# 64-row parts of q, k and v in one group per token tile, and the weights of k issued sooner, in a transformer block

## The chip, the cores and the metric

The kernel runs on one core of a Trainium2 chip. The metric is the device time of one execution in microseconds; the median of several runs is given.

## What is computed

The block works on two sequences (B = 2) of 2048 tokens with 576 features, 16 heads of 36, in float32. Cut to what matters here:

```python
xn = _ln(x, 1e-06)
xn = xn * (1 + sc_msa[:, None, :]) + sh_msa[:, None, :]
qkv = (xn @ w_qkv + b_qkv).reshape(B, N, 3, H, hd)
q, k, v = (qkv[:, :, 0], qkv[:, :, 1], qkv[:, :, 2])
q = _ln(q, 1e-05, qn_g, qn_b)
k = _ln(k, 1e-05, kn_g, kn_b)
attn = softmax(einsum('bqhd,bkhd->bhqk', q, k) * hd ** (-0.5))
o = einsum('bhqk,bkhd->bqhd', attn, v).reshape(B, N, C) @ w_proj + b_proj
x = x + g_msa[:, None, :] * o
# ... then a second normalisation, a two-layer MLP and its gated residual
```

The shifts, scales and gates come from silu(c) @ w_ada + b_ada.

## The kernel before, in words

The two sequences (batches) are taken one after the other. For each there is a stage that makes q, k and v (`inputs`), a stage of attention (`attend`), and a stage of the output projection (`outputs`); the MLP of both follows at the end. The change is in `inputs` and in what it calls.

**Tiles and products.** `inputs` goes over 16 token tiles of 128 tokens. A tile's normalised rows lie in `xnt` by feature: 576 features are four chunks of 128 and one of 64, and the last chunk is there twice, in rows 0 to 63 and 64 to 127. Each of q, k and v is a product of 128 tokens by 576 columns, in two halves of 288 columns, each half in a PSUM bank of its own. `whole` (matmul at line 379) does the four full chunks of both halves, and in the trace it is 16 instructions, since a float32 matmul has two. `halved` (line 390) does the 64-row chunk: the first half on rows 0 to 63, the second on rows 64 to 127, four instructions that run in pairs side by side. `two_products` (line 394) puts them in turn: products with an even number do `whole` and then `halved`, odd ones `halved` and then `whole`, so that the 64-row parts of two neighbours come together.

**The rest of a tile.** For each tile t the loop at line 946 does q, k and v with `two_products`. VectorE adds the bias `bq` while it takes the result out of PSUM (line 960 for q and k into `both`, line 967 for v). After q it does `head_scale` of tile t-1 (line 892: a reduction on VectorE, a square root on ScalarE, a reciprocal, and a multiplication on GpSimd). After k in even tiles, and after q in odd ones, come three things: `input_by_feature` (line 851), which transposes the normalised rows of tile t+1 on TensorE (lines 357, 358) and modulates them on ScalarE (line 365); `by_feature` of tile t-2 (line 910), nine transposes of q and k (line 915), taken out of PSUM by VectorE and ScalarE; and `next_rows` (line 941), which loads and normalises tile t+2 (`rows_normed`, line 269, with a square root on ScalarE in its midst). At the end of the tile `centred` (line 877) subtracts the mean of each head on VectorE and squares on ScalarE.

**Order and buffers.** The stage has four PSUM buffers of two banks (`s_tile`, line 86). A tile takes six: q, k, v, one for the transposes of the next tile, two for `by_feature`. VectorE keeps the order of the program in this stage (line 1176); the order of the other engines is set by a scheduler by program order and readiness, and it also picks which buffer an allocation takes. After tiles 3, 7, 11, 13 and 15, `by_feature` gathers a block of keys with DMAs on SP's queue (`take_k_block`, line 806), and VectorE works on it (`parted`, line 787) in the `by_feature` that follows.

**Weights.** `input_weights` (line 825) loads them on SP's queue: q in two parts, then the 64-row chunk of all three, then x tiles 1 and 2 of batch 0 (the argument `then`, given at line 1172), the bias `bq`, k, and v. For batch 1 it is called ahead of `outputs` of batch 0, with no x tiles.

Of the kernel before, what the change touches and what calls it, by code (L numbers as in the profile page):

```python
# [8 lines left out]
F32 = mybir.dt.float32  # L9
# [3 lines left out]
ALU = mybir.AluOpType  # L13
# [3 lines left out]
P = 128  # L17
# [5 lines left out]
FULL = 4  # L23
# [8 lines left out]
def dit_block(  # L32
# [25 lines left out]
    nc = tc.nc  # L58
# [27 lines left out]
    def s_tile():  # L86
        return psum["s"].tile([P, 2, 512], F32, tag="s", name="s")
# [35 lines left out]
    def halves(ap):  # L123
        return ap.rearrange("p (a f) -> p a f", a=2)
# [224 lines left out]
        nc.vector.tensor_copy(xn[:, C:], xn[:, 512:576])  # L349
        return xn[:, :512], xn[:, 512:]  # L350

    def transposed(src, tail):

        ps = s_tile()
        t4, t1 = ps[:, 0, :], ps[:, 1, :]
        for k in range(FULL):
            nc.tensor.transpose(t4[:, k * P : (k + 1) * P], src[:, k * P : (k + 1) * P], ident)  # L357
        nc.tensor.transpose(t1[:, :P], tail, ident)  # L358
        return t4, t1

    def modulated(dst, src, which, b):

        t4, t1 = transposed(*src)
        for k in range(NKC):
            nc.scalar.activation(  # L365
                dst[:, k, :],
                t4[:, k * P : (k + 1) * P] if k < FULL else t1[:, :P],
                AF.Identity,
                bias=mod[:, which, k, b : b + 1],
                scale=mod[:, which + 1, k, b : b + 1],  # L370
            )
# [15 lines left out]
    def halved(outs, stationary, moving, first):  # L387
        for a in range(2):
            r = slice(64 * a, 64 * a + 64)
            nc.tensor.matmul(  # L390
                outs[a], stationary(FULL, a)[r], moving(FULL, a)[r], start=first, stop=not first
            )

    def two_products(outs, stationary, moving, turn):


        parts = (whole, halved) if turn % 2 == 0 else (halved, whole)
        for part in parts:
            part(outs, stationary, moving, part is parts[0])
# [325 lines left out]
    def block_of_small():  # L725
# [96 lines left out]
            for a in range(2):  # L822
                nc.sync.dma_start(out=dst[64 * a : 64 * a + 64, :, :], in_=src[:, :, a, :])

        def input_weights(then=lambda: None):
            pool, close = opened("wq")
            wq = pool.tile([P, FULL, 3 * C], F32, name="wq")
            wq4 = pool.tile([P, 3, HALF], F32, name="wq4")
            bq = pool.tile([P, 3 * C], F32, name="bq")
            for f0, n in ((0, HALF), (HALF, HALF), (C, C), (2 * C, C)):  # L830
                f = slice(f0, f0 + n)
                nc.sync.dma_start(out=wq[:, :, f], in_=w_qkv[0:512, f].rearrange("(k p) f -> p k f", p=P))
                if f0 == HALF:
                    last_chunk(wq4, w_qkv, 3, HALF)
                    then()
                    nc.sync.dma_start(out=bq, in_=b_qkv.partition_broadcast(P))
            return (wq, wq4, bq), close

        def tile_loaded(src, queue):
            xt = xs["tiles"].pop(0)  # L840
            xs["tiles"].append(xt)
            queue.dma_start(out=xt[:, :C], in_=src)
            return xt
# [4 lines left out]
        def input_rows(b, t, queue):  # L848
            return tile_normed(tile_loaded(x[b, t * P : (t + 1) * P, :], queue))

        def input_by_feature(b, rows):
            xnt = xs["pool"].tile([P, NKC, P], F32, name="xnt", bufs=2)
            modulated(xnt, rows, 0, b)
            return xnt

        def first_modulated():
# [11 lines left out]
        def inputs(b, weights, work, xnt, loaded):  # L868
# [5 lines left out]
            def banks_of_two():  # L874
                return [bank for ps in (s_tile(), s_tile()) for bank in (ps[:, 0], ps[:, 1])]
# [16 lines left out]
            def head_scale(t, both, parts=((0, 2),)):  # L892
                var = work.tile([P, 2 * H], F32, name="var")
                for w0, w1 in parts:
                    nc.vector.tensor_reduce(
                        var[:, w0 * H : w1 * H],
                        squares["sq"][:, w0 * C : w1 * C].rearrange("p (h d) -> p h d", d=HD),
                        AX.X,
                        ALU.add,
                    )  # L900
                nc.scalar.activation(var, var, AF.Sqrt, bias=eps5, scale=1.0 / HD)
                inv = work.tile([P, 2 * H], F32, name="inv")
                nc.vector.reciprocal(inv, var)
                heads = both.rearrange("p (h d) -> p h d", d=HD)
                nc.gpsimd.tensor_tensor(
                    heads, heads, inv.unsqueeze(2).to_broadcast([P, 2 * H, HD]), ALU.mult
                )
                normed[t] = both

            def by_feature(t, banks, chunks=range(NQK), all_on_vector=False):  # L910
                both, begun = normed[t], [*taken]
                taken.clear()
                parts = [(c, banks[i // 4][:, i % 4 * P : i % 4 * P + P]) for i, c in enumerate(chunks)]
                for c, ps in parts:
                    nc.tensor.transpose(ps, both[:, c * P : (c + 1) * P], ident)  # L915

                for c, ps in parts[::-1]:
                    dst = chunk(c, slice(t * P, (t + 1) * P))
                    if c < 4 and not all_on_vector:
                        nc.scalar.activation(  # L920
                            dst, ps, AF.Identity, bias=bias_qk[:, c : c + 1], scale=gain_qk[:, c : c + 1]
                        )
                    else:
                        nc.vector.tensor_scalar(
                            dst, ps, gain_qk[:, c : c + 1], bias_qk[:, c : c + 1], ALU.mult, ALU.add
                        )
                for do in begun:
                    do()
                if t == TPB - 1:
                    taken.append(take_q(0, 0))  # L930
                if t + 1 in key_tiles and NQK - 1 in chunks:
                    i = key_tiles.index(t + 1)
                    taken.append(take_k_block(*key_tiles[i - 1 : i + 1]))
# [7 lines left out]
            def next_rows(t):  # L941
                return tile_normed(loaded.pop(0)) if loaded else input_rows(b, t, nc.sync)

            rows = next_rows(1)
            before = None
            for t in range(NT):
                both = work.tile([P, 2 * C], F32, name="both", bufs=3)
                for w in range(3):
                    ps = s_tile()
                    two_products(  # L950
                        [ps[:, a, :HALF] for a in range(2)],
                        lambda k, a: xnt[:, k, :],
                        lambda k, a: (
                            wq[:, k, w * C + a * HALF : w * C + (a + 1) * HALF] if k < FULL else wq4[:, w, :]
                        ),
                        3 * t + w,
                    )
                    bias = halves(bq[:, w * C : (w + 1) * C])
                    if w < 2:
                        nc.vector.tensor_tensor(  # L960
                            halves(both[:, w * C : (w + 1) * C]), ps[:, :, :HALF], bias, ALU.add
                        )
                        if w == 0 and t > 0:
                            head_scale(t - 1, before)
                    else:
                        heads = "p a (h d) -> p a h d"
                        nc.vector.tensor_tensor(
                            vv[:, t, :, 0:HD].rearrange("p (a h) d -> p a h d", a=2),
                            ps[:, :, :HALF].rearrange(heads, d=HD),
                            bias.rearrange(heads, d=HD),  # L970
                            ALU.add,
                        )

                    if w == (1 if t % 2 == 0 else 0):
                        if t + 1 < NT:
                            ahead = input_by_feature(b, rows)
                        if t >= 2:
                            by_feature(t - 2, banks_of_two())
                        if t + 2 < NT:
                            rows = next_rows(t + 2)  # L980

                    if t == NT - 1 and w < 2:
                        centred(both, w, w + 1)
                    if t == NT - 1 and w == 1:
                        head_scale(t, both, ((0, 1), (1, 2)))
                if t + 1 < NT:
                    centred(both)
                before, xnt = both, ahead
# [119 lines left out]
        def outputs(b, weights, between, scratch):  # L1108
# [60 lines left out]
        xnt = first_modulated()  # L1169
        loaded = []  # L1170
        weights, close_weights = input_weights(
            lambda: loaded.extend(tile_loaded(x[0, t * P : (t + 1) * P, :], nc.sync) for t in (1, 2))
        )
        for b in range(B):
            work, close_work = opened("work", side="right")
# [439 lines left out]
```

## Time and profile before

| | us |
|---|---|
| median of 3 runs | 3229.54 |
| lowest and highest | 3227.64, 3229.89 |
| the profiled execution, its own time | 3230.55 |
| its span in the profile | 3228.7 |
| TensorE busy with matmuls | 3205.6 |
| line 379 in all, with wq | 392.9 |
| line 390 in all, with wq | 59.6 |

The profile names each group of instructions by line, engine and operation, with the tile written, the tiles read, the shape and the count. "Busy" counts matmuls from the start to an end that is modelled, and they overlap: the distance between two starts says what one costs. A row of the order of time has its start, its duration, the instruction and its count, and in brackets how long the engine was idle before and what released it. The q, k, v stage of batch 0 starts with line 379 at 19.83 us, that of batch 1 at 1117.97 us.

### The profile page before, as it was taken

To read this page: it belongs to the slowest core of one execution; us is meant where nothing else is said; L and a number is where in the kernel's file an instruction comes from. 1 tells how busy PE (TensorE), PEld (TensorE's weight loads), DVE (VectorE), ACT (ScalarE), POOL (GpSimd) and SP (SyncE) were. 2 spreads that over 40 slices of the span, in tenths; PEclk is the share of its full clock that TensorE was granted. 3 is DMA by queue.
4 is the path that set the end of the run, shared out by engine and by line. 5 is a ranking of instruction groups with operands and counts; after the bars stand their busy time and mean duration, and the time that the engine had idled before them with its cause. 6 is when DMAs were issued, how large, how long until landed. Compare 5 with 4: busy or idle time off the path is not lost.

```text
span 3228.7 us, 46968 instructions
## 1 busy us (share of the span) xinstructions
PE 3205.6 (99%) x18143; PEld 1883.0 (58%) x18143; DVE 1451.2 (45%) x2131; ACT 1496.8 (46%) x2952; POOL 355.1 (11%) x432
## 2 busy tenths in 40 slices
PE   8999999999999999999999999999999999999999
PEld 5775333333333777733333333358888888777777
DVE  4674333333333366633333333345555544455454
ACT  2335666666666033366666666633555552000000
POOL 1111000112110111100001111010000000111111
PEclk9999999999999999999999999999999999999999
DMA  3112212223231400122222223154322223433331
GB/s 131 26 26 65 76 35 68 66 70 83 69 85 34 146 26 24 27 56 46 50 44 65 68 66 74 47 173 156 120 90 88 93 80 110 153 132 111 118 103 38
DMA packets 129332, 253.16 MB, mean 78 GB/s; under 512 B 22979, under 2 KB 68492, under 8 KB 127052
## 3 DMA queue, kind: packets, MB, share of 16 engines
q1 hardware_dynamic: 105588, 182.07, 18.5%
q0 software_dynamic: 22640, 66.23, 7.4%
q8 instruction: 145, 2.38, 0.3%
q10 hardware_dynamic: 872, 1.77, 0.2%
q14 instruction: 87, 0.71, 0.1%
HBM read 135.40 MB, written 66.35 MB: 62 GB/s over the span
## 4 chain that ended last, share of the span: by engine, by line
PE 99%; DMA 1%; SPq 0%; DVE 0%; issue 0%; DVEq 0%
PE b L1025 28%; PE b L1012 19%; PE s L379 16%; PE s L1527 15%; PE m L1368 12%; PE s L390 2%; PE m L1382 2%; PE one L1368 2%; PE s L915 1%; PE s L357 1%; PE t L1428 0%; DMA wq<-in_w_qkv_dram 0%; DMA wa<-in_w_ada_dram 0%; PE b L192 0%; PE b L915 0%; DMA km<-qo 0%
## 5 line engine op out<-in xcount | busy, mean ns | idle before, releaser
L1016 ACT ACTIVATE pt<-b 128x512 f32<-128x512 f32 x2048 | 1057.4, 608 | 485.6 <-PE b L1025 270.8
L1025 PE MATMUL b<-pt,vt 128*64 128x512 f32 x4096 | 935.0, 598 | 0.0
L1025 PEld LDWEIGHTS b<-pt,vt 128*64 128x64 f32 x4096 | 271.9, 136 | 582.0 <-issue 438.8
L1012 PE MATMUL b<-qm,km 32*128 32x512 f32 x4096 | 566.5, 614 | 0.2 <-DMA km<-qo 0.2
L1073 DVE TENSOR_TENSOR ot<-b,ot 128x512 f32<-128x512 f32 x192 | 132.8, 691 | 653.2 <-PE b L1025 652.7
L1012 PE MATMUL b<-qe,ke 16*128 16x512 f32 x2048 | 422.8, 790 | 0.0
L379 PE MATMUL s<-wq,xnt 128*128 128x288 f32 x1536 | 392.9, 411 | 3.9 <-DMA wq<-in_w_qkv_dram 3.2
L1527 PE MATMUL s<-ws,as 128*128 128x288 f32 x1440 | 351.8, 406 | 0.0
L1012 PEld LDWEIGHTS b<-qm,km 32*128 32x128 f32 x4096 | 191.6, 184 | 269.3 <-ACT pt L1016 205.0
L379 PEld LDWEIGHTS s<-wq,xnt 128*128 128x128 f32 x1536 | 286.4, 191 | 95.5 <-issue 18.9
L1527 PEld LDWEIGHTS s<-ws,as 128*128 128x128 f32 x1440 | 273.6, 190 | 75.6
L1044 DVE RECIPROCAL den<-den 128x512 f32<-128x512 f32 x64 | 213.6, 3337 | 12.3 <-DMA den<-den_dram 12.3
L1368 PE MATMUL m<-xnt,wb 128*128 128x256 f32 x864 | 213.8, 383 | 0.0
L1368 PE MATMUL m<-s,wb 128*128 128x256 f32 x864 | 210.1, 379 | 0.2 <-DVE s L1338 0.2
L1071 DVE COPY ot<-b 128x512 f32<-128x512 f32 x64 | 44.3, 692 | 334.7 <-PE b L1025 334.7
L1368 PEld LDWEIGHTS m<-xnt,wb 128*128 128x128 f32 x864 | 159.1, 190 | 32.2 <-issue 11.9
L1368 PEld LDWEIGHTS m<-s,wb 128*128 128x128 f32 x864 | 164.1, 190 | 22.9 <-DVE s L1338 0.6
L1012 PEld LDWEIGHTS b<-qe,ke 16*128 16x128 f32 x2048 | 108.1, 184 | 114.4 <-issue 113.0
L1395 DVE TENSOR_TENSOR cs<-m,cs 128x512 f32<-128x512 f32 x72 | 49.7, 690 | 213.1 <-ACT cs L1394 151.7
L1527 PE MATMUL s<-ws,hidden 128*128 128x288 f32 x576 | 142.3, 406 | 0.0
L1505 DVE TENSOR_TENSOR as<-hidden 128x1152 f32<-128x1152 f32 x80 | 139.0, 1801 | 0.0
L365 ACT ACTIVATE xnt<-s,mod 128x128 f32<-128x128 f32 x180 | 66.8, 460 | 152.7 <-PE s L358 152.7
(174 smaller groups left out, 2553.5 us busy)
## 6 DMA issues: line engine op xcount, KB each, us to landing
gelu<-cs SPq DMA_DIRECT2D x144, 256.0 KB
hidden<-gelu SPq DMA_DIRECT2D x16, 2304.0 KB
den<-den_dram SPq DMA_DIRECT2D x128, 128.0 KB
x_dram<-kr POOLq DMA_DIRECT2D x48, 288.0 KB, 2.8
qm<-qo SPq DMA_DIRECT2D x192, 64.0 KB
kr<-in_x_dram POOLq DMA_DIRECT2D x32, 288.0 KB, 3.8
xr<-x_dram SPq DMA_DIRECT2D x32, 288.0 KB
out_dram<-y POOLq DMA_DIRECT2D x30, 288.0 KB, 3.8
```

Source lines behind the costliest of these rows:

```text
L365: nc.scalar.activation(dst[:, k, :], t4[:, k * P : (k + 1) * P] if k < FULL else t1[:, :P], AF.Identity, bias=mod[:, which, k, b : b + 1], ...
L379: nc.tensor.matmul(outs[a], stationary(k, a), moving(k, a), start=(first and k == 0), stop=(not first and k == FULL - 1),)
L390: nc.tensor.matmul(outs[a], stationary(FULL, a)[r], moving(FULL, a)[r], start=first, stop=not first)
L1012: nc.tensor.matmul(ps, k[r, keys], q[r, :], start=first, stop=not first)
L1016: nc.scalar.activation(pt[:, h, :], banks[2 * c + h], AF.Exp, scale=SCALE)
L1025: nc.tensor.matmul(acc[64 * h : 64 * h + 64, :], vt[:, v0 : v0 + 64], pt[:, h, :], start=pt is pts[0][0], stop=pt is pts[-1][0],)
L1044: nc.vector.reciprocal(den, den)
L1073: nc.vector.tensor_tensor(ot, acc, ot, ALU.add)
L1368: nc.tensor.matmul(out_m[m], wb[:, slot[m], k, f * P : (f + 1) * P], moving[m](k), start=k == 0 and (m == 1 or (first and m in (2, 5, 6))) ...
L1382: nc.tensor.matmul(out_m[m], w[r, f * P : (f + 1) * P], a[r, FULL, t * PAIR : (t + 1) * PAIR], start=first and m != 4, stop=not first and ...
L1505: nc.vector.tensor_tensor(stationary[m], x_, y_, op)
L1527: nc.tensor.matmul(ms[m], stationary[m][:, f, :], ws[m][:, f, :], start=(f == 0), stop=(f == HF - 1))
```

## The change

Tiles 0 to 13 get a loop of their own. In it q does `whole`; the transposes of the next tile follow; k does `whole`; then the three `halved` parts of q, k and v come one after the other; and v does `whole`. In tile 0 of batch 0 k's `whole` stands ahead of the transposes. `next_rows` comes right after the transposes, `head_scale` after the biases of q and k, and `by_feature` of tile t-2 after v's bias, at the end of the tile. Tiles 14 and 15 keep the old order. In four tiles (0 and 9 of batch 0, 0 and 1 of batch 1) the fifth transpose gets a PSUM buffer of its own (`apart`). In `input_weights`, k's weights are issued ahead of x tile 1, `bq` and x tile 2, which keep that order among themselves and stand ahead of v's weights.

```diff
-    def transposed(src, tail):
+    def transposed(src, tail, apart=False):
         ps = s_tile()
-        t4, t1 = ps[:, 0, :], ps[:, 1, :]
+        t4, t1 = ps[:, 0, :], (s_tile() if apart else ps)[:, 1, :]
...
                 nc.sync.dma_start(out=wq[:, :, f], in_=w_qkv[0:512, f].rearrange("(k p) f -> p k f", p=P))
                 if f0 == HALF:
                     last_chunk(wq4, w_qkv, 3, HALF)
-                    then()
+                if f0 == C:
+                    then(1)
                     nc.sync.dma_start(out=bq, in_=b_qkv.partition_broadcast(P))
+                    then(2)
...
-            for t in range(NT):
+            for t in range(NT - 2):
+                both = work.tile([P, 2 * C], F32, name="both", bufs=3)
+                q, q_parts = product(0, xnt)
+                whole(*q_parts, True)
+                behind = b == t == 0
+                if behind:
+                    k, k_parts = product(1, xnt)
+                    whole(*k_parts, True)
+                ahead = input_by_feature(b, rows, t in ((0, 9), (0, 1))[b])
+                rows = next_rows(t + 2)
+                if not behind:
+                    k, k_parts = product(1, xnt)
+                    whole(*k_parts, True)
+                v, v_parts = product(2, xnt)
+                halved(*q_parts, False)
+                halved(*k_parts, False)
+                halved(*v_parts, True)
+                biased(0, q, t, both)
+                biased(1, k, t, both)
+                if t > 0:
+                    head_scale(t - 1, before)
+                whole(*v_parts, False)
+                biased(2, v, t, both)
+                if t >= 2:
+                    by_feature(t - 2, banks_of_two())
+                centred(both)
+                before, xnt = both, ahead
+            for t in range(NT - 2, NT):
                 both = work.tile([P, 2 * C], F32, name="both", bufs=3)
                 for w in range(3):
-                    ps = s_tile()
-                    two_products(
...
+                    ps, parts = product(w, xnt)
+                    two_products(*parts, 3 * t + w)
+                    biased(w, ps, t, both)
+                    if w == 0:
+                        head_scale(t - 1, before)
```

`product` allocates a PSUM buffer and gives the halves with their operands; `biased` is the bias step that stood in the loop.

More of the change, by code (lines that the diff above doesn't have):

```diff
@@ L359, in transposed, with modulated @@
         return t4, t1
-    def modulated(dst, src, which, b):
-        t4, t1 = transposed(*src)
+    def modulated(dst, src, which, b, apart=False):
+        t4, t1 = transposed(*src, apart)
         for k in range(NKC):
@@ L823, in last_chunk, with input_weights @@
                 nc.sync.dma_start(out=dst[64 * a : 64 * a + 64, :, :], in_=src[:, :, a, :])
-        def input_weights(then=lambda: None):
+        def input_weights(then=lambda t: None):
             pool, close = opened("wq")
@@ L849, in input_rows, with input_by_feature @@
             return tile_normed(tile_loaded(x[b, t * P : (t + 1) * P, :], queue))
-        def input_by_feature(b, rows):
+        def input_by_feature(b, rows, apart=False):
             xnt = xs["pool"].tile([P, NKC, P], F32, name="xnt", bufs=2)
-            modulated(xnt, rows, 0, b)
+            modulated(xnt, rows, 0, b, apart)
             return xnt
@@ L942, in next_rows, with product, biased @@
                 return tile_normed(loaded.pop(0)) if loaded else input_rows(b, t, nc.sync)
+            def product(w, xnt):
+                ps = s_tile()
+                return ps, (
+                    [ps[:, a, :HALF] for a in range(2)],
+                    lambda k, a: xnt[:, k, :],
+                    lambda k, a: (
+                        wq[:, k, w * C + a * HALF : w * C + (a + 1) * HALF] if k < FULL else wq4[:, w, :]
+                    ),
+                )
+            def biased(w, ps, t, both):
+                bias = halves(bq[:, w * C : (w + 1) * C])
+                if w < 2:
+                    nc.vector.tensor_tensor(halves(both[:, w * C : (w + 1) * C]), ps[:, :, :HALF], bias, ALU.add)
+                else:
+                    heads = "p a (h d) -> p a h d"
+                    nc.vector.tensor_tensor(
+                        vv[:, t, :, 0:HD].rearrange("p (a h) d -> p a h d", a=2),
+                        ps[:, :, :HALF].rearrange(heads, d=HD),
+                        bias.rearrange(heads, d=HD),
+                        ALU.add,
+                    )
@@ L947, in inputs @@
+            for t in range(NT - 2, NT):
                 both = work.tile([P, 2 * C], F32, name="both", bufs=3)
                 for w in range(3):
-                    ps = s_tile()
-                    two_products(
[L951 to L972, printed above, removed]
+                    ps, parts = product(w, xnt)
@@ L976, in inputs @@
                             ahead = input_by_feature(b, rows)
[L977 to L980, printed above, removed]
+                        by_feature(t - 2, banks_of_two())
                     if t == NT - 1 and w < 2:
@@ L1171, in block_of_small @@
         weights, close_weights = input_weights(
-            lambda: loaded.extend(tile_loaded(x[0, t * P : (t + 1) * P, :], nc.sync) for t in (1, 2))
+            lambda t: loaded.append(tile_loaded(x[0, t * P : (t + 1) * P, :], nc.sync))
         )
```

## The prediction

> **What bounds the kernel now.** I read the page first, then TensorE's own groups with the shapes kept apart, then the order of time in the stage that the diff touches, then who waits for whom. The page says that TensorE carries the whole span:
>
> ```profile
> PE 3205.6 (99%) x18143; PEld 1883.0 (58%) x18143; DVE 1451.2 (45%) x2131; ACT 1496.8 (46%) x2952; POOL 355.1 (11%) x432
> ...
> L379 PE MATMUL s<-wq,xnt 128*128 128x288 f32 x1536 | 392.9, 411 | 3.9 <-DMA wq<-in_w_qkv_dram 3.2
> ```
>
> Only about 23 us of the span are free of matmuls, so the change can win idle time at the start, or make TensorE's stream itself shorter. The second row holds the one long wait of the q, k, v stage, 3.2 us for the weights. For the stream, two token tiles of batch 1 in order of time (start, duration, engine, line):
>
> ```profile
> 1142.46 8.03 PE L379 MATMUL s<-wq,xnt 128*128 128x288 f32 x32
> 1150.42 1.24 PE L390 MATMUL s<-wq,xnt 64*128 64x288 f32 x8
> 1151.59 4.15 PE L379 MATMUL s<-wq,xnt 128*128 128x288 f32 x16
> 1155.58 0.60 PE L357 MATMUL s<-ident,xt 128*128 128x128 f32 x4
> 1156.01 0.27 PE L358 MATMUL s<-ident,xt 128*128 128x128 f32 x1
> 1156.12 1.15 PE L915 MATMUL s<-ident,both 128*128 128x128 f32 x9
> 1157.11 4.05 PE L379 MATMUL s<-wq,xnt 128*128 128x288 f32 x16
> 1161.08 1.24 PE L390 MATMUL s<-wq,xnt 64*128 64x288 f32 x8
> ...
> 1171.74 1.24 PE L390 MATMUL s<-wq,xnt 64*128 64x288 f32 x8
> 1172.91 7.30 PE L379 MATMUL s<-wq,xnt 128*128 128x288 f32 x29
> ```
>
> There is no idle note on any of these rows: the stage is a closed stream, 1172.91 - 1142.46 = 30.45 us per two tiles. To be seen: three x8 groups per two tiles, and a full-height run that follows one is longer (4.15) than one that follows transposes (4.05).
>
> **The price of a group.** A full-height matmul takes a slot of (4.05 - 0.406)/15 = 0.243 us (0.406 is the duration of one, 15 the steps between starts). A transpose takes 0.109: five at line 357/358 and nine at line 915 start at 1155.58 and are over at 1157.11, 1.53/14. The eight 64-row instructions of a group are four pairs that run side by side. Two tiles hold 96 full-height slots, 12 pairs and 28 transposes: 108 x 0.2425 + 28 x 0.109 = 29.25. The 1.20 that is left, over three groups, is 0.40 us per group: the price of going to 64-row parts and back. A longer group must not cost more for this to count. The output stage has groups of eight pairs:
>
> ```profile
> 1089.60 2.21 PE L390 MATMUL s<-wp,qo 64*128 64x288 f32 x16
> ...
> 1091.74 15.79 PE L379 MATMUL s<-wp,qo 128*128 128x288 f32 x64
> ```
>
> From its start to the next full-height one this group takes 2.14, the x8 group at 1150.42 takes 1.17. The four further pairs cost 0.97, which is four slots and nothing else.
>
> **What the Trainium skill says.** "TensorEngine Tiling (Array Packing)", Key Properties: "Mode switching requires drain", changing the tiling mode drains TensorE. The trace agrees and puts 0.40 us on a round trip. "TensorE: Matmul & The Clock Gate", Part 3, says that matmuls on different row groups run concurrently: agrees, a pair fills one slot. The same page, Part 1, says that TensorE falls to half clock after an idle window of some 3.4 us and returns after as much busy time. The trace agrees at the start (clock 0.82 and 0.84 in the two stretches below). "DMA: Bandwidth & Descriptors", Queues, rings and completion order: on each DMA engine, descriptors of a queue are consumed in ring order. So what is issued ahead of the weights of k on SP's queue delays them.
>
> **Part 1, fewer groups.** Before, 48 products of a batch give 24 groups (x384 at line 390 over both batches is 48 groups of 8). After, tiles 0 to 13 have one group of six pairs each, tiles 14 and 15 keep their three: 17 per batch. Fourteen groups fewer in all, the 64-row work being the same: 14 x 0.40 = 5.6 us, all on the path, since TensorE has no idle time there. The new tile is then 48 + 6 slots, 14 transposes and 0.40: 15.02 us instead of 15.22.
>
> **Part 2, k's weights.** The start before, in order of time:
>
> ```profile
> 19.83 4.12 PE L379 MATMUL s<-wq,xnt 128*128 128x288 f32 x16 [0.76 <-ACT xnt L859]
> 23.88 1.24 PE L390 MATMUL s<-wq,xnt 64*128 64x288 f32 x8
> 28.28 5.79 PE L379 MATMUL s<-wq,xnt 128*128 128x288 f32 x16 [3.16 <-DMA wq<-in_w_qkv_dram]
> 33.91 0.60 PE L357 MATMUL s<-ident,xt 128*128 128x128 f32 x4
> 34.34 0.27 PE L358 MATMUL s<-ident,xt 128*128 128x128 f32 x1
> 34.45 4.05 PE L379 MATMUL s<-wq,xnt 128*128 128x288 f32 x16
> ```
>
> and by stretches (DMA share and GB/s are the last columns, the clock before them):
>
> ```profile
> 25.00:30.00 5.00, 1.84 (x6) 1.29 (x5) 0.76 (x1) 0.00 (x0) 0.00 (x0) 0.82 1.06 392
> 30.00:35.00 5.00, 5.00 (x22) 3.88 (x21) 0.89 (x2) 0.34 (x1) 0.00 (x0) 0.84 0.16 59
> ```
>
> k waits until 28.28, and the cold clock then makes its 16 slots take 33.91 - 28.28 = 5.63 instead of 3.88. Two x tiles (288 KB each) and bq (864 KB) go ahead of k now and behind it after: 1440 KB = 1.47 MB less at 392 GB/s is 3.76 us, so k lands at about 24.5. The bound on this: at best TensorE is simply ready, at 23.75; at worst the slowest of the DMA engines sets it and half is won, 26.4. In the new order tile 0 does q, k (24.5 to 28.4), the transposes of tile 1 (to 28.95), the six pairs, then v. The gap before k is 0.8 us, too short to lose the clock.
>
> What is late next is v: all that was ahead of v's weights still is, so they land when they did. The stretches show DMA full to about 30.5, so I take 31.0. Also, with the added tile ("apart") q, k and the two transposed parts fill the four PSUM buffers, and v's pairs wait for ScalarE's modulation, 1.86 us from 29.15: v's first pair at about 30.8, its full-height part at 31.4. Before, v's part began at 34.45 with v's two pairs still to do. Gain 34.45 - 31.4 = 3.05, and 2 x 0.2425 = 0.5 for the pairs: 3.5 us. Ends: 2.0 (v late by 1.5 more) and 4.2 (no PSUM wait).
>
> **What is moved, and its cover.** x tile 1 lands behind k, at some 25.3; its normalisation takes 2.2 us on VectorE and ScalarE (22.38 to 24.6 now), ready by 27.6, and is wanted at 28.45. bq lands at about 27.5, wanted at 30. x tile 2 lands at 28.3; its normalisation stands ahead of q's bias on VectorE, so q's buffer is free only at about 33, which no one needs before 35. If these covers were gone, each microsecond would be one on the path. In batch 1 the weights are issued from 1060.1 to 1065.5 and first used at 1117.97: 52 us of cover, cost nothing.
>
> In the steady tile, next_rows (an x load on SP, statistics on VectorE, a square root on ScalarE) moves ahead of q's bias, and by_feature to the end of the tile. VectorE keeps the order of the program, so the loop counts: bias of v and the wait for transposes 1.0, five evictions 1.8, centring 3.0, then ScalarE's square 1.2, modulation 1.9 and root 0.3, then 0.8 to finish the rows, biases of q and k 1.5, reduction 1.3, root 0.4, reciprocal 0.4: 13.6 of 15.0 us. It closes, with 1.4 to spare. PSUM: q's buffer is free some 3 us before the by-feature transposes want one, k's 4, and the transposes' own 2.4 us before the next k wants one. So I put these at nothing, upper end 0.2 us per tile. The key blocks' DMAs on SP (five issues of 0.6 to 0.8, landing 5.4 at the median) now have 10.6 instead of 20 us before VectorE's next use at tile 14, and 15 at tiles 6 and 10: still covered by 2 to 4 us.
>
> **The sum.** 5.6 + 3.5 = 9.1 us. Against the profiled execution's own 3230.55 (span 3228.7, 1.85 around it) that is 3221.4; the median of the runs is 3229.54, 1.0 lower, and the same gain puts it at 3220.4.
>
> **The rivals.** (a) The start does not gain: k lands no sooner, or v's weights take over the wait. For it: DMA is full from 5 to 30 us, and v cannot come sooner. Against it: v's first use was at 34.45, 3 us after the queue ran dry. It gives 3229.5 - 5.6 = 3223.9. (b) TensorE begins to wait in each tile, for a PSUM buffer or VectorE, 0.2 us in 28 tiles: 5.6 back, 3226.0. For it: four PSUM buffers and six allocations a tile, and a scheduler that picks the buffer; against it: the slacks above. The same time would come if the change did not do what it says, the switch being paid per product and not per group: only 3.5 won. The x16 group speaks against that. (c) Slower: VectorE's ordered loop, with ScalarE's three steps in it, comes out longer than the tile. It decides from 15.0 us, and for a loss of 0.2% it has to reach about 15.9: 28 x 0.9 less the buffers' slack of 2 x 4 is 17, more than 9.1 + 6.5. At 16.2 us the kernel takes 3229.5 - 9.1 + 25 = 3246. For it: queued behind the new wait for next_rows' root on VectorE are both biases, the head scaling and v's bias, and TensorE waits for v's buffer. Against: it would need 2.3 us more than the rows show.
>
> **How the numbers follow.** As reckoned, 3218 to 3223: 0.72. (a) 0.08. (b) and the switch paid per product 0.13. (c) 0.07. About 0.2%, 6.5 us or 3223.1, is what a measurement can tell from no change. Faster gets the forecast and a little of (a): 0.74; same the rest of (a) and (b): 0.19; slower 0.07. The range goes from 3217.5 (all of the start's upper end) to 3226.5, which takes in (a) and most of (b).
>
> **What would show it.** Right: line 390's rows as x12 groups, 34 groups in all; tiles of 15.0 us; the wait for wq ahead of k under 1 us and no stretch at a low clock near 30; v's full-height part at about 31.4. Wrong: idle notes on line 379, 358 or 915 by VectorE or ScalarE in tiles 2 to 13, tiles over 15.2 us, or k still waiting past 26.

## The result and the profile after

The changed kernel takes 3220.86 us (median of 13 runs, 3219.57 to 3223.11); the kernel before, measured beside it, 3229.32 (3227.05 to 3231.25). The ratio is 0.9975, 95% interval 0.9968 to 0.9983: 8.5 us faster, where 9.1 was forecast and 3220.4 given. The interval's upper end, 0.17%, is just under the 0.2% that the prediction took as distinguishable, so the sign is sure and the size is known to some 2.5 us. The profiled executions differ by 9.7 (3230.55 and 3220.86).

The page after, for the same two rows:

```profile
PE 3199.1 (99%) x18143; PEld 1883.2 (59%) x18143; DVE 1452.6 (45%) x2131; ACT 1495.2 (46%) x2952; POOL 355.2 (11%) x432
...
L379 PE MATMUL s<-wq,xnt 128*128 128x288 f32 x1536 | 391.4, 408 | 1.9 <-DMA wq<-in_w_qkv_dram 1.1
```

The same 18143 matmuls, and 6.5 us less of busy time; the wait for the weights is 1.1 instead of 3.2. A token tile of batch 1 after, in order of time:

```profile
1154.26 4.05 PE L379 MATMUL s<-wq,xnt 128*128 128x288 f32 x16
1158.14 0.60 PE L357 MATMUL s<-ident,x_first 128*128 128x128 f32 x4
1158.58 0.27 PE L358 MATMUL s<-ident,x_first 128*128 128x128 f32 x1
1158.69 4.05 PE L379 MATMUL s<-wq,xnt 128*128 128x288 f32 x16
1162.66 1.73 PE L390 MATMUL s<-wq,xnt 64*128 64x288 f32 x12
1164.32 4.15 PE L379 MATMUL s<-wq,xnt 128*128 128x288 f32 x16
1168.30 1.15 PE L917 MATMUL s<-ident,both 128*128 128x128 f32 x9
1169.29 0.89 PE L379 MATMUL s<-wq,xnt 128*128 128x288 f32 x3
```

One x12 group, no idle note on any row, and 1169.29 - 1154.26 = 15.03 us for the tile (15.22 before, 15.02 forecast). The start after, in order of time and then by stretches:

```profile
18.79 4.12 PE L379 MATMUL s<-wq,xnt 128*128 128x288 f32 x16 [0.76 <-ACT xnt L861]
24.01 4.15 PE L379 MATMUL s<-wq,xnt 128*128 128x288 f32 x16 [1.10 <-DMA wq<-in_w_qkv_dram]
27.99 0.60 PE L357 MATMUL s<-ident,xt 128*128 128x128 f32 x4
28.43 0.27 PE L358 MATMUL s<-ident,xt 128*128 128x128 f32 x1
28.63 1.24 PE L390 MATMUL s<-wq,xnt 64*128 64x288 f32 x8
30.19 0.76 PE L390 MATMUL s<-wq,xnt 64*128 64x288 f32 x4 [0.31 <-ACT xnt L365]
30.87 8.03 PE L379 MATMUL s<-wq,xnt 128*128 128x288 f32 x32
```

```profile
25.00:30.00 5.00, 4.87 (x27) 3.42 (x25) 2.53 (x8) 1.91 (x6) 0.00 (x0) 1.00 1.05 394
30.00:35.00 5.00, 4.81 (x21) 3.59 (x22) 2.08 (x4) 0.91 (x4) 0.00 (x0) 1.00 0.43 157
```

k begins at 24.01 (before 28.28), at full clock (1.00 where it was 0.82 and 0.84), and v's full-height part at 30.87 (before 34.45). The wait ahead of k is 1.10 us, a little over the 1 us that was forecast as its upper end. The only new wait is that of v's pairs for ScalarE (line 365, the modulation).

By stages, from the first full-height part of q to the first scores of attention: batch 0 took 246.28 before and takes 240.42; batch 1 took 241.32 (1117.97 to 1359.29) and takes 238.40. Every later stage is as it was, within 0.1 us: the output projection of batch 0 took 72.04 and takes 72.03, and all from the second output projection to the end of the span 1096.64 and 1096.62. The two stages are 5.86 and 2.92 us shorter, 8.8 in all. The rest of the 9.7 lies ahead of the stage: q starts at 18.79 where it started at 19.83. The change does not touch what comes before q, and in the executions below that start lies anywhere from 18.61 to 21.20.

### The profile page after: what moved, and what is told of

The parts are those of the page before. It is cut to its first block, busy times and chain, and to the rows that moved or that the text cites. A ratio compares the mean times of both kernels' runs of the same rounds, so it can differ in the third digit from the quotient of the medians.

```text
span 3219.0 us, 46999 instructions
## 1 busy us (share of the span) xinstructions
PE 3199.1 (99%) x18143; PEld 1883.2 (59%) x18143; DVE 1452.6 (45%) x2131; ACT 1495.2 (46%) x2952; POOL 355.2 (11%) x432
## 3 DMA queue, kind: packets, MB, share of 16 engines
q10 hardware_dynamic: 872, 1.77, 0.2%
## 4 chain that ended last, share of the span: by engine, by line
PE 99%; DMA 1%; SPq 0%; DVE 0%; issue 0%; ACT 0%; DVEq 0%
PE b L1062 28%; PE b L1049 19%; PE s L379 16%; PE s L1564 15%; PE m L1405 12%; PE s L390 2%; PE m L1419 2%; PE one L1405 2%; PE s L917 1%; PE s L357 1%; PE t L1465 0%; DMA wq<-in_w_qkv_dram 0%; PE b L192 0%; PE b L917 0%; DMA km<-qo 0%; PE s L358 0%
## 5 line engine op out<-in xcount | busy, mean ns | idle before, releaser
L379 PEld LDWEIGHTS s<-wq,xnt 128*128 128x128 f32 x1536 | 284.6, 190 | 86.5 <-issue 13.5
L1443 ACT ACTIVATE cs<-cs,b_sb 128x512 f32<-128x512 f32 x144 | 98.8, 719 | 68.2 <-DVE cs L1438 31.4
```

Source lines behind the costliest of these rows:

```text
L379: nc.tensor.matmul(outs[a], stationary(k, a), moving(k, a), start=(first and k == 0), stop=(not first and k == FULL - 1),)
L1443: nc.scalar.activation(part, part, AF.Gelu, bias=b1_sb[:, g : g + 1])
```

## The experiments

Their times stand beside runs of the kernel before, whose median was 3229.0 in the first four and 3228.7 in the second four. A distance to after is one of medians from different series, in each of which the kernel before lay within 0.7 us.

**Tiles only.** The new loop, with the weights in the old order:

```diff
                 if f0 == HALF:
                     last_chunk(wq4, w_qkv, 3, HALF)
-                if f0 == C:
                     then(1)
-                    nc.sync.dma_start(out=bq, in_=b_qkv.partition_broadcast(P))
                     then(2)
+                    nc.sync.dma_start(out=bq, in_=b_qkv.partition_broadcast(P))
```

> The new tile loop with the old order of the weights (x tiles 1 and 2 and bq ahead of k). Theory: 0.40 us per group, 14 groups fewer, 5.6 us; but the wait for k stays, at a cold clock, and the one group that used to run inside that wait (q and k of tile 0) now comes after it, 1.45 of slots and 0.40 of switching, less the 0.5 of v's pairs: 4.2 us of gain, 3225.1. Rival 1, the two parts add up without touching each other: 5.6 us, 3223.7. Rival 2, the number of groups costs nothing and all of the gain is the weights: 3229 or above. In either of the first two the second batch's stage, q to first scores, is 2.8 to 2.9 us shorter than before.

Measured: 3225.9, ratio 0.9989 (0.9981 to 0.9998), 3.1 us faster than before. Batch 1's stage is 238.39 (after 238.40), which refutes the second rival. The start of batch 0:

```profile
18.61 4.12 PE L379 MATMUL s<-wq,xnt 128*128 128x288 f32 x16 [0.76 <-ACT xnt L860]
27.38 5.84 PE L379 MATMUL s<-wq,xnt 128*128 128x288 f32 x16 [4.66 <-DMA wq<-in_w_qkv_dram]
...
33.69 1.24 PE L390 MATMUL s<-wq,xnt 64*128 64x288 f32 x8
```

The wait is 1.50 us longer (4.66 against 3.16): the group of 64-row parts no longer lies in it (1.17), and q began 1.22 sooner in this execution, while k's weights landed 0.90 sooner. The clock falls as it did before (5.84 for the 16 slots). From k's start to v's full-height part it is 8.56 us (35.94 less 27.38) where it was 6.17, and only 0.5 of that is v's pairs: the new order alone makes the start 1.9 us worse, the way the theory had it. The gain is nearer to 4.2 than to 5.6, though the interval (0.6 to 6.1 us) does not shut 5.6 out. The traces speak for the theory: batch 0's first scores come 1.84 us sooner (264.27 against 266.11) and batch 1's stage is 2.93 shorter, 4.8 in all, of which 0.9 is k's weights landing sooner.

**Weights only.** The kernel before, with k's weights ahead of x tiles 1 and 2 and bq (the `input_weights` of the change).

> The old tile loop with k's weights ahead of the x tiles and bq. Theory: k lands some 3.2 to 3.8 us sooner, by which time q's and k's pairs have run, so k waits hardly or not at all and the clock stays up; v's full-height part then waits for its own weights until about 31: gain 3.4 us, 3225.9, and the gains of this run and of the tiles alone come to less than the whole change brings. Rival, v's weights are not what comes next: v starts right after the transposes at about 29.5, gain 5 us, 3224.4. In both the second batch's stage is as long as before, 241.3 us.

Measured: 3227.25, ratio 0.9995 (0.9986 to 1.0003); 1.75 us, which by itself can't be told from nothing and is half of what was expected. The trace shows the mechanism: k starts right behind the pairs, and v waits for its own weights.

```profile
24.42 1.24 PE L390 MATMUL s<-wq,xnt 64*128 64x288 f32 x8
25.59 4.15 PE L379 MATMUL s<-wq,xnt 128*128 128x288 f32 x16
29.58 0.60 PE L357 MATMUL s<-ident,xt 128*128 128x128 f32 x4
30.02 0.27 PE L358 MATMUL s<-ident,xt 128*128 128x128 f32 x1
30.48 4.12 PE L379 MATMUL s<-wq,xnt 128*128 128x288 f32 x16 [0.20 <-DMA wq<-in_w_qkv_dram]
```

v's weights are there at about 30.4; 31.0 was taken. Batch 1's stage is 241.34, as before. In this execution q starts late, at 20.38: the matmuls ahead of it (the 20 of line 192) take 3.57 us where they take 2.21 after. The two parts alone bring 3.1 + 1.75 = 4.9 us, the whole 8.5; their intervals are too wide to tell this from a plain sum. By the traces, one execution of each, batch 0's first scores come 1.84 and 3.89 us sooner with one part alone, 5.73 together, and 6.90 sooner with both (266.11 before, 264.27, 262.22, and 259.21 after). That is 1.2 us more than the sum, where the forecast of 9.1 is 1.5 over the sum of the two expectations (4.2 and 3.4), but k's landing alone moves by as much between executions (below).

**Two groups per tile.** v's 64-row parts behind its full-height ones; everything is computed as in after:

```diff
-                halved(*v_parts, True)
...
-                whole(*v_parts, False)
+                whole(*v_parts, True)
+                halved(*v_parts, False)
```

> After, but with v's 64-row parts behind its full-height ones: each of tiles 0 to 13 has a group of four pairs and one of two, 28 groups more in all, with the same matmuls. Theory (a fixed price per group): 28 x 0.40 = 11.2 us slower than after, 3232.1, so slower than before as well by 2.8 us. Rival, the price goes with the products and not with the groups: as after, 3220.9. The second batch's stage, 238.4 us after, becomes 244.0 by the theory.

Measured: 3231.74, ratio 1.0008 (1.0000 to 1.0016), 10.9 us over after. The price goes with the groups. A tile in order of time:

```profile
1181.48 4.05 PE L379 MATMUL s<-wq,xnt 128*128 128x288 f32 x16
1185.46 1.24 PE L390 MATMUL s<-wq,xnt 64*128 64x288 f32 x8
1186.63 4.15 PE L379 MATMUL s<-wq,xnt 128*128 128x288 f32 x16
1190.71 0.76 PE L390 MATMUL s<-wq,xnt 64*128 64x288 f32 x4
1191.39 1.20 PE L917 MATMUL s<-ident,both 128*128 128x128 f32 x9
...
1196.86 3.32 PE L379 MATMUL s<-wq,xnt 128*128 128x288 f32 x13
```

From k's part to the next tile's k it is 1196.86 - 1181.48 = 15.38, 0.35 over the 15.03 of after, for one group more. Batch 1's stage is 243.41, 5.0 over after for 14 groups (0.36 each), where 5.6 was expected: the added group, which has transposes behind it, costs 0.35, not 0.40.

**No tile with `apart`.** The fifth transpose shares the buffer in all tiles.

```diff
-                ahead = input_by_feature(b, rows, t in ((0, 9), (0, 1))[b])
+                ahead = input_by_feature(b, rows)
```

> After, with no tile's fifth transpose in a PSUM buffer of its own. Theory: at the start v's pairs find a free buffer and no longer wait for ScalarE's modulation; up to 0.6 us is won there if v's weights have landed by then, nothing if not; in the other tiles the slack of the buffers hides the other assignment: 3220.3 to 3220.9. Rival: the extra buffers are what keeps the assignment free of waits, and without them TensorE waits for a buffer in many tiles, 0.2 us in 28 tiles or more: 3226 or above.

Measured: 3223.46, ratio 0.9983 (0.9976 to 0.9990), 2.6 us over after: neither theory. The intervals of the two ratios overlap, so the trace has to carry the reading; its span is 2.2 us longer. At the start v's pairs indeed no longer wait (one x12 group at 29.29), so it was the buffer that they waited for. No tile waits for a buffer, and batch 1's stage is 238.40. The loss is at the end of the stage, where attention takes over PSUM. From the list of TensorE's waits, and the two places in order of time:

```profile
PE b L1049 <- DVE vt L963: 1.7, 2, 1.4
```

```profile
260.71 1.12 PE L1049 MATMUL b<-qm,km 32*128 32x512 f32 x5 [1.36 <-DVE vt L963]
```

```profile
1352.24 0.77 PE L1049 MATMUL b<-qm,km 32*128 32x512 f32 x3 [0.30 <-DVE vt L963]
```

The scores wait until VectorE has taken v of tile 15 out of PSUM: the first ones in batch 0, the third in batch 1. After, they start ahead of that instruction:

```profile
259.21 1.14 PE L1049 MATMUL b<-qm,km 32*128 32x512 f32 x8
...
259.89 0.69 DVE L963 TENSOR_TENSOR vt<-s,bq 128x576 f32<-128x576 f32 x1
```

So after, the first scores are not in the banks of that product. That the extra buffers do this by shifting which buffer each later product gets is inferred: the profile does not show the bank of a tile. Batch 0's wait is 1.36 us. Batch 1 takes 773.80 from its first scores to its projection, the wait of 0.30 in it, 0.97 more than after; the other executions take 772.72 to 773.27. Together that is 2.3 of the 2.6 us.

**The 64-row chunk's weights behind k's.**

```diff
-                if f0 == HALF:
-                    last_chunk(wq4, w_qkv, 3, HALF)
                 if f0 == C:
+                    last_chunk(wq4, w_qkv, 3, HALF)
                     then(1)
```

> After, with the 64-row chunk's weights (two DMAs of 216 KB) issued behind k's. Theory: k's wait of 1.1 us goes (432 KB at 392 GB/s are 1.1 us), but v's own weights, which land at about 30.5 in the run with the weights alone, come next: v's full-height part at 30.5 instead of 30.9, 0.4 us won, 3220.5. Rival: v's weights land earlier than that and all of it is won: 1.1 us, 3219.8. Either is near what the times can tell; the start of v's full-height part in the trace decides.

Measured: 3220.52, ratio 0.9976 (0.9966 to 0.9985): as after. In the trace k isn't waited for, but q started late, at 20.37, and v's full-height part came at 31.08, behind the same 0.31 us of waiting for ScalarE. Neither expectation's start of v (30.5, or sooner) is seen, and with q 1.6 us later than in after this execution doesn't tell them apart.

**v's weights ahead of bq and x tile 2**, with the same move of the chunk's weights:

```diff
                 if f0 == C:
+                    last_chunk(wq4, w_qkv, 3, HALF)
                     then(1)
-                    nc.sync.dma_start(out=bq, in_=b_qkv.partition_broadcast(P))
-                    then(2)
+            nc.sync.dma_start(out=bq, in_=b_qkv.partition_broadcast(P))
+            then(2)
```

> After, with the order q, k, 64-row chunk, x tile 1, v, bq, x tile 2. Theory: v's weights no longer come last, 1152 KB sooner by 3 us, so neither k's nor v's weights are waited for; what remains is the normalisation of x tile 1 and v's PSUM buffer: v's full-height part at about 29.8, 1.1 us won over after, 3219.8. Rival: q's bias now waits for bq and x tile 2 and holds its buffer until 34, and TensorE waits for a buffer in tile 1: nothing won, or up to 1 us lost, 3221 to 3222.

Measured: 3221.34, ratio 0.9975 (0.9966 to 0.9984). The trace follows the theory: v's full-height part at 29.76, no wait for either weights, none in tile 1, and batch 0's stage 239.29, 1.1 shorter than after. The median doesn't show it, so it can't be called better than after.

```profile
27.52 1.24 PE L390 MATMUL s<-wq,xnt 64*128 64x288 f32 x8
29.08 0.76 PE L390 MATMUL s<-wq,xnt 64*128 64x288 f32 x4 [0.32 <-ACT xnt L365]
29.76 8.03 PE L379 MATMUL s<-wq,xnt 128*128 128x288 f32 x32
```

With the weights out of the way it is v's PSUM buffer, held until ScalarE has modulated, that is last.

**More work in VectorE's ordered chain.** The reduction of `head_scale` is repeated (it writes the same values again):

```diff
-                for w0, w1 in parts:
+                for w0, w1 in parts * (2 if t < NT - 3 else 1):
                     nc.vector.tensor_reduce(
```

> After, with the reduction of head_scale done twice in tiles 0 to 12 of both batches, one more VectorE instruction of 1.34 us in the ordered chain of each tile. Theory: the chain has 1.4 us to spare in a tile of 15.0 (VectorE waits 1.5 us ahead of v's bias in the trace of after), so nothing: 3220.9. Rival, VectorE's chain already sets the pace somewhere: 26 x 1.4 less some slack, up to 3250.

Measured with 2: 3222.57, ratio 0.9981 (0.9974 to 0.9988), 1.7 us over after, which the overlapping intervals leave in doubt. In the tiles it costs nothing (batch 1's stage is 238.40). TensorE has one wait that after lacks, 1.27 us, in tile 14 of batch 0; ahead of that VectorE has normalised more rows than in other tiles, with three tiles' statistics begun between 218.80 and 220.79. That the one leads to the other is likely, and not shown.

> After, with the same reduction done four times, 4.1 us more in each of 26 tiles. Theory: the chain becomes 13.6 + 4.1 = 17.7 us, 2.7 longer than the tile; less the buffers' slack of 2 x 4 us, 26 x 2.7 - 8 = 62 us slower than after: 3283. If the trace's two waits (1.5 ahead of v's bias, 0.7 ahead of q's) are both slack, the chain is 12.9 and the price 26 x 2.0 - 8 = 44: 3265. Rival: VectorE's order doesn't reach TensorE at all, since four buffers decouple them: 3220.9.

Measured with 4: 3236.74, ratio 1.0024 (1.0015 to 1.0034), 15.9 us over after: slower than before, by the mechanism of rival (c), but a quarter to somewhat over a third of what was expected (62 and 44). VectorE's rows of one tile:

```profile
1198.32 0.69 DVE L963 TENSOR_TENSOR vt<-s,bq 128x576 f32<-128x576 f32 x1
...
1205.21 0.16 DVE L278 RECIPROCAL rstd<-std 128x1 f32<-128x1 f32 x1 [0.77 <-ACT std L276]
1205.41 0.58 DVE L279 TENSOR_SCALAR xt<-xt,mv,rstd 128x576 f32<-128x576 f32 x1
1205.91 1.42 DVE L960 TENSOR_TENSOR both<-s,bq 128x576 f32<-128x576 f32 x2
1207.24 5.51 DVE L897 TENSOR_REDUCE var<-sq 128x32 f32<-128x1152 f32 x4
1213.26 0.35 DVE L905 RECIPROCAL inv<-var 128x32 f32<-128x32 f32 x1 [0.52 <-ACT var L903]
1213.53 0.69 DVE L963 TENSOR_TENSOR vt<-s,bq 128x576 f32<-128x576 f32 x1
```

From v's bias to v's bias it is 1213.53 - 1198.32 = 15.21, and nowhere in it does VectorE wait for TensorE: this is the chain's own length, 0.18 over TensorE's 15.03. The three repeats are 5.51 x 3/4 = 4.1 of it, so without them it is 11.1 us long, not 13.6. In a tile in which VectorE also works on a block of keys it is longer: in batch 0 v's biases are at 126.23 and 143.65, 17.4 us apart, and TensorE's first wait, 1.69 us for the second of them, comes right there (144.40, shown in the last section). Seven waits for VectorE or for the steps behind it, 12.0 us in all, and the low clock after two of them make up most of the 15.9.

**Both kernels once more, for the start.** One execution each; a single run of before beside them took 3231.21.

> The kernel before, once more, for its start alone. Theory: the wait for k ends at 28.0 to 28.6 us whenever q started, since DMA sets it, and v's full-height part starts at 34.5 if the clock falls in that wait and at about 32.8 if it doesn't (16 slots at full clock instead of 5.6 us); the price of the cold clock, 1.7 us, is then not in every run, and that is why the median of before lies 1 to 1.5 us under its profiled run. Rival: the clock falls in every run, and v's full-height part starts at 34.3 to 34.7 again.

Before, again 3230.26 us:

```profile
21.20 5.81 PE L379 MATMUL s<-wq,xnt 128*128 128x288 f32 x16 [0.75 <-ACT xnt L859]
...
28.92 4.15 PE L379 MATMUL s<-wq,xnt 128*128 128x288 f32 x16 [0.73 <-DMA wq<-in_w_qkv_dram]
```

k waits until 28.92, later than the 28.0 to 28.6 expected, and v's full-height part is at 33.45, between the two expectations. The half clock did not fall in the wait here. It fell in q, and k's 16 slots then ran at full clock: from k to v's part it is 4.53 us where it was 6.17, so the price of the low clock is 1.64, as reckoned. The whole is hardly shorter (by 0.3), because k landed 0.64 later and attention of batch 1 took 0.5 longer (773.27 against 772.77).

> The kernel after, once more, for its start alone. Theory: k's full-height part at 24.0 to 24.6 us or, if q starts late, right behind q; v's full-height part at 30.8 to 31.3 either way, set by x tile 1, the modulation and v's buffer. Rival: it moves with q's start, by up to 1.6 us.

After, again 3220.19: q from 19.39, k right behind it, v's full-height part at 30.32, a little ahead of the range expected, and not moved by q's start.

## Why the prediction was right, point by point

**Fewer groups: right, and shown.** 0.40 us per group and 14 groups were 5.6 us. Batch 1, which has no start of its own, gives seven of them clean: 241.32 - 238.40 = 2.92, against 2.8. The two-group kernel moves the time back nearly by its number of groups (10.9 us for 28). That the price is a fixed one per group, and not per pair or product, was read from the x16 groups of the output stage. The x12 groups confirm it: 1164.32 - 1162.66 = 1.66 for six pairs, 0.49 more than the 1.17 of four, which is two slots.

**k's weights: right in kind, the sum near.** k at 24.5 was forecast and is at 24.01. v at 31.4 was forecast, behind ScalarE's modulation, and is at 30.87 behind that very wait; its weights were reckoned to land at 31.0 and land at about 30.4. In the profiled pair the start gives 34.45 - 30.87 + 0.5 = 4.1 us, for 3.5. With the 2 x 2.92 = 5.8 of the groups that is 9.9, for the 9.7 between the two profiled executions. The medians are 1.2 us less apart, and before's two profiled executions lie 1.3 and 1.5 us over its median of 3229.0. The theory that this is the half clock falling into the wait is not borne out: in the second execution it fell elsewhere, v's part came 1.0 us sooner, and the time was the same within 0.3. The traces offer another candidate, not shown for the runs without a trace: in the old order k's wait ended at 27.38 (tiles only), 28.28 and 28.92 in three executions, and each microsecond of this is one of the start's gain. What makes the medians closer stays open; the start is worth 2.7 (8.5 less 5.8) to 4.1 us.

The step "the gap before k is 0.8 us, too short to lose the clock" came out right here (1.10 us, at full clock), but not as a rule: in other executions the clock fell with no longer pause ahead (last section). In this it had some luck.

**What was put at nothing.** The key blocks, x tile 1 and bq were covered, as said: x tile 1 was there at 24.73, wanted at 27.99, and no TensorE row of tiles 2 to 13 has an idle note. But two sizes were off. VectorE's chain was reckoned at 13.6 of 15.0 us, and is 11.1. The step added ScalarE's square, modulation and root to VectorE's instructions as if each waited for the one before; in the trace VectorE does its statistics while ScalarE squares, and only 0.77 and 0.52 us of waiting for ScalarE stay in the chain. So rival (c) needed 3.9 us more and not 1.4 in most tiles. In those with a block of keys, whose work the sum left out, it needed 1.7 (17.4 less the 4.1 of the repeats is 13.3). And `apart` was counted only as a cost at the start (0.6 us, correctly: from the pairs' start at 28.63 to 30.87 it is 2.24, an x12 group takes 1.66). What it is worth, some 2.3 to 2.6 us at the two handovers to attention, was not seen, since the working followed the PSUM buffers within the stage and stopped at its end.

**The rivals.** (a), no gain at the start, is refuted by the trace, not by the weights-only run alone, whose interval holds zero. (b), waits in each tile: none. The switch being paid per product: refuted by the two-group kernel. (c) exists as a mechanism, as the four reductions show; it begins at the 15.0 us that were named, and the distance to them was taken too small.

## What to carry to other kernels

Here matmuls that use part of the rows were best gathered: the price of the change of mode went by the round trip, and could be read beforehand from a stage that has longer groups. When a load is moved ahead, write down what each later load and each buffer then ends, since the next limit may be close: here v's weights (30.4) and the buffer of v's pairs (30.19) lay within a microsecond. Work out two parts of a change together, as their gains need not add up. And a rotation of PSUM buffers has to be followed into the next stage: where the last product sits can decide when that stage may start.

## What the runs showed of the hardware

A round trip to 64-row parts costs 0.40 us between full-height matmuls, and 0.35 for the group of the two-group kernel that transposes follow. TensorE's clock fell to half after shorter pauses than the 3.4 us that the Trainium skill's page "TensorE: Matmul & The Clock Gate", Part 1, names for an idle window. With four reductions, pauses of 1.69, 1.70 and 1.77 us left the clock alone, and those of 2.42 and 2.46 brought it down. One of each:

```profile
144.40 0.66 PE L357 MATMUL s<-ident,xt 128*128 128x128 f32 x4 [1.69 <-DVE vt L963]
...
162.79 5.53 PE L379 MATMUL s<-wq,xnt 128*128 128x288 f32 x16 [2.42 <-ACT qo L922]
```

5.53 us for 16 slots (5.83 after the pause of 2.46), where 4.05 to 4.15 is usual: a pause of 2.4 us cost 1.4 to 1.8 us more than itself. At the start of the kernel the length of one pause doesn't decide. In the two-group kernel no pause from 13.5 us on is longer than 0.79, and the clock is 0.50 from 21 to 23 us:

```profile
19.96 9.69 PE L379 MATMUL s<-wq,xnt 128*128 128x288 f32 x32 [0.79 <-ACT xnt L861]
```

9.69 us for 32 slots that usually take 8.03, while the wait of 1.10 in after left the clock at 1.00. In two executions of before the low clock fell into k's slots, behind a wait of 3.16, and into q's. In the second of these it cost nothing: q took 1.7 us longer, and k had to wait 0.73 us for its weights all the same.
